# Sums of values through DRAM by blocks, and a new order of the pieces around the attention steps

## The chip, the cores and the metric

One core of a Trainium2 chip. The metric is device time in microseconds (us) of one execution. A median is over the executions of one kernel, and ratios compare fast executions of two kernels that ran in the same rounds on the same chip.

## The reference, cut to what matters

Two layers on x of 16 batches, 1024 rows and 256 columns, all in fp32. The first layer is a graph convolution with two matrix products and batch norms, a residual and a layer norm. The second one, which the change concerns, is attention whose queries come from a gated graph product:

```python
c_adj = mean(x, axis=channel)
Wg    = adj * (gate of c_adj[m] - c_adj[n])       # 1024 x 1024 per batch: the "gate rows"
g     = relu(einsum('bcn,bnm->bcm', fea, Wg) * para)   # "graph"; gives the queries
k, v  = split(x @ kv_w)                           # "keys", "values"
attn  = softmax(q @ k.T * scale)                  # 4 heads of 64
out   = attn @ v                                  # "sums of values", o
x     = layernorm(x + out)
```

## The kernel before: the parts that matter

The kernel holds scores and sums of values with the head's channels on the partitions. Each batch is 16 steps: scores of step g+1, exponentials (ScalarE), acc sums of the exponentials (VectorE), and sums of values of step g. Four steps make a turn; at the head of a turn stand "pieces", given to slots by `put(batch, slot, piece, ...)`. A turn has two slots, a batch eight. I call a batch's turns the first to the fourth. The same engine queues run scores, pieces and the preparation of the next two batches, each strictly in the order in which the program records it.

```python
def attend(g):
    ...
    if cp == NT // 2 - 1:                      # a pair of heads is complete: after 4 steps
        t = otp.tile([P, FB], F32, tag=f"ot{pair}", bufs=2 - pair, name=f"ot{g}")
        nc.scalar.copy(t, o[0]); nc.vector.tensor_add(t, o[1], t)
        OT[b, hf, pair] = t

def finish_a(b, j):                            # 64 of these: 2 x 128 rows each
    p = ps_t.tile([P, 2, C], F32, tag="t", name="pf")
    for a in range(2):
        for pair in range(NP):
            nc.tensor.transpose(p[:, a, ts(pair, P)], OT[b, hf, pair][:, ts(k + a, P)], ident)
    nc.vector.tensor_mul(r, p, rd)             # divide by the softmax sum (views cut here)
    (nc.gpsimd if b < B - 1 else nc.vector).tensor_add(r, r, x1s.pop((b, j)))
...
WG = (2, 3, 2, 1)        # gate rows per slot
QG = (6, 6, 6, 7, 7)     # graph pieces per slot, the last five slots
order = (dens, recips, finish_a, finish_b, x1_v, rows, ln1_a, ln1_b, put_x1, get_x1, finish_s, means, load, crow)
```

`dens` (tile pd) needs all acc sums of a half batch. `finish_s` takes the layer norm statistics of r, `finish_b` scales and stores the result, `means` and `crow` (tile pc) prepare the next batch's gate, `load` and `bn2_q` fetch and scale the rows of the batch after it.

## Time and profile before

| quantity | before |
|---|---|
| time, median | 2536.4 us (4 runs, 2535.86 to 2539.2) |
| span of the profiled run | 2538.7 us |
| TensorE, VectorE, ScalarE, GpSimd busy | 97%, 70%, 41%, 35% |
| a batch in the steady part | 104.10 us |
| first to fourth turn | 25.24, 24.93, 27.33, 26.61 us |

A turn is measured between the starts of its first TensorE group and the next turn's first group, averaged over twelve batches. That distance is cost on TensorE; the durations in its rows overlap and are not. The lines themselves are in the prediction.

### The profile page before, as it was taken

What the parts mean: (1) busy time and instruction counts of PE and PEld (TensorE: products, weight loads), DVE (VectorE), ACT (ScalarE), POOL (GpSimd) and SP (SyncE); (2) the same over time, 40 slices, a digit from 0 to 9 for tenths busy, and PEclk for the clock granted to TensorE, in tenths of its full rate; (3) what the DMA queues carried; (4) which work ended last, traced back from release to release, by engine and by line L of the source; (5) the groups of instructions that cost most, each with busy time, mean ns of one, the idle gap of its engine ahead of it and who ended that gap; (6) DMA issues with size and microseconds to landing.
All of it is one profiled execution on the core that took longest, in us unless ns stands there. A gap on an engine that the chain in (4) does not pass through costs nothing. (4 is left out here: it accounts for less than half of the span.)

```text
span 2538.7 us, 33394 instructions
## 1 busy us (share of the span) xinstructions
PE 2471.2 (97%) x12573; PEld 1048.0 (41%) x12573; DVE 1765.1 (70%) x2654; ACT 1042.9 (41%) x1325; POOL 876.9 (35%) x766
## 2 busy tenths in 40 slices
PE   8999999998998799999999999999999999999997
PEld 4444444443444333443434434444444344443432
DVE  5545554556767676877778778788687786877656
ACT  2000000004452355463554645646455465554644
POOL 2222223222565222433334324344243342432132
PEclk9999999999999899999999999999999999999998
DMA  3122212230785322223222221232222312222000
GB/s 133 66 83 100 100 66 83 100 115 38 273 326 183 60 57 59 51 59 67 47 55 59 58 64 43 55 69 53 63 46 54 76 38 63 47 59 63 9 14 23
DMA packets 392711, 195.27 MB, mean 77 GB/s; under 512 B 265320, under 2 KB 380640, under 8 KB 385376
## 3 DMA queue, kind: packets, MB, share of 16 engines
q1 hardware_dynamic: 392544, 193.08, 27.0%
q8 instruction: 101, 1.65, 0.3%
q14 instruction: 66, 0.54, 0.1%
HBM read 114.31 MB, written 78.71 MB: 76 GB/s over the span
## 5 line engine op out<-in xcount | busy, mean ns | idle before, releaser
L775 ACT ACTIVATE e<-s 128x1024 f32<-128x1024 f32 x512 | 496.3, 1020 | 537.1 <-PE s L763 488.5
L784 DVE TENSOR_TENSOR acc<-acc,e 128x1024 f32<-128x1024 f32 x384 | 522.2, 1360 | 73.1 <-ACT e L775 41.7
L763 PE MATMUL s<-qT,kT 64*64 64x512 f32 x4096 | 495.6, 599 | 14.8 <-ACT e L775 13.3
L794 PE MATMUL o<-e,v 64*64 64x512 f32 x4096 | 486.8, 590 | 0.0
L737 PE MATMUL pg<-wg,x 128*128 128x512 f32 x960 | 429.0, 595 | 0.0
L846 POOL TENSOR_TENSOR r<-r,x 128x512 f32<-128x512 f32 x60 | 115.7, 1928 | 555.5 <-DVE r L841 352.2
L763 PEld LDWEIGHTS s<-qT,kT 64*64 64x64 f32 x4096 | 147.7, 133 | 312.1 <-issue 251.3
L794 PEld LDWEIGHTS o<-e,v 64*64 64x64 f32 x4096 | 157.1, 133 | 285.1 <-issue 276.5
L602 POOL TENSOR_TENSOR yt<-yt,stq 128x512 f32<-128x512 f32 x120 | 188.6, 1572 | 248.5 <-DMA yt<-yT 243.8
L737 PEld LDWEIGHTS pg<-wg,x 128*128 128x128 f32 x960 | 175.5, 190 | 207.8 <-issue 198.2
L101 ACT COPY u<-pa 128x512 f32<-128x512 f32 x15 | 8.8, 586 | 475.3 <-PE pa L306 475.3
L704 DVE SCALAR_TENSOR_TENSOR wg<-wg,adj_sb 128x1024 f32<-128x1024 f32 x128 | 156.6, 1241 | 57.3 <-ACT wg L700 55.0
L306 PE MATMUL pa<-AhT,x 128*128 128x512 f32 x360 | 161.8, 592 | 0.0
L712 PE MATMUL pk<-x1T,kvw 128*128 128x512 f32 x256 | 118.4, 606 | 1.3 <-DVE x1T L663 1.3
L862 ACT ACTIVATE r<-r,nm,rs_z 128x256 f32<-128x256 f32 x128 | 69.8, 594 | 121.2 <-POOL nm L854 121.2
L723 PE MATMUL pv<-kvw,x1T 128*128 128x256 f32 x512 | 115.8, 380 | 0.8 <-ACT kT L715 0.8
L337 PE MATMUL ph<-agg,SW 128*128 128x512 f32 x240 | 112.8, 592 | 0.0
L306 PE MATMUL pa<-T,sx 128*128 128x512 f32 x240 | 107.9, 592 | 0.0
L745 DVE TENSOR_TENSOR qT<-pg,para_sb 128x512 f32<-128x512 f32 x64 | 44.2, 690 | 86.9 <-PE pg L737 86.9
L306 PEld LDWEIGHTS pa<-AhT,x 128*128 128x128 f32 x360 | 68.4, 190 | 86.1 <-issue 86.1
L723 PEld LDWEIGHTS pv<-kvw,x1T 128*128 128x128 f32 x512 | 94.9, 190 | 14.6 <-ACT kT L715 1.6
L482 PE MATMUL po<-hL,SV 128*128 128x512 f32 x224 | 98.4, 592 | 0.0
(193 smaller groups left out, 3113.6 us busy)
## 6 DMA issues: line engine op xcount, KB each, us to landing
h<-hT SPq DMA_DIRECT2D x28, 1024.0 KB, 4.4
hL<-h SPq DMA_DIRECT2D x28, 1024.0 KB, 9.4
x<-in_x_dram SPq DMA_DIRECT2D x16, 1024.0 KB, 7.2
yT<-y SPq DMA_DIRECT2D x64, 256.0 KB, 2.6
out_dram<-r SPq DMA_DIRECT2D x64, 256.0 KB, 2.2
xr<-in_x_dram SPq DMA_DIRECT2D x62, 256.0 KB, 2.9
yt<-yT SPq DMA_DIRECT2D x240, 64.0 KB, 2.2
x<-x SPq DMA_DIRECT2D x120, 128.0 KB, 2.0
```

The source lines that it names most:

```text
L306: nc.tensor.matmul(p, xs[n][:, k, :], bs[n][:, k, :], start=(k == 0), stop=(k == KN - 1))
L337: nc.tensor.matmul(p, ws[n][:, ts(f, P)], bs[n], start=True, stop=True)
L602: nc.gpsimd.tensor_tensor(y, y, sc, op)
L704: nc.vector.scalar_tensor_tensor(t, t, 1.0, adj_sb[:, i, :], op0=OP.add, op1=OP.mult)
L712: nc.tensor.matmul(p, kvw[:, k, ts(c, P)], x1Ts[b][:, k, ts(h, FB)], start=(k == 0), stop=(k == CT - 1))
L723: nc.tensor.matmul(p[:, ts(a, C)], x1Ts[b][:, k, ts(j + a, P)], kvw[:, k, C:], start=(k == 0), stop=(k == CT - 1),)
L737: nc.tensor.matmul(pg[b], x1s[b, k // 2][:, k % 2, ts(c, P)], wgs[b, k][:, ts(h, FB)], start=(k == 0), stop=(k == NT - 1))
L763: nc.tensor.matmul(t[r * HD : (r + 1) * HD, h, :], kTs[b, pair][h * HD : (h + 1) * HD, ts(2 * cb + r, HD)], qTs[b, pair, hf][h * HD : (h + ...
L775: nc.scalar.activation(E[g, a], S.pop((g, a)), AF.Exp)
L784: nc.vector.tensor_add(ACC[b, hf, pair], ACC[b, hf, pair], E[g, a])
L794: nc.tensor.matmul(O[b, hf, pair][r][h * HD : (h + 1) * HD, :], vs[b][r * HD : (r + 1) * HD, cb, pair * P + h * HD : pair * P + (h + 1) * HD],
L846: (nc.gpsimd if b < B - 1 else nc.vector).tensor_add(r, r, x1s.pop((b, j)))
```

## The change

Its intent: take the transposes of the sums of values off TensorE, by writing the sums to DRAM and fetching them back in 32x32 blocks, which VectorE can turn; and place pieces so that an engine does not stand behind another's result. The core of the diff (DRAM declarations, comments and helper lines cut):

```diff
-                t = otp.tile([P, FB], F32, tag=f"ot{pair}", bufs=2 - pair, name=f"ot{g}")
+                t = otp.tile([P, FB], F32, tag=f"ot{pair}", bufs=1, name=f"ot{g}")
...
-                OT[b, hf, pair] = t
+                if by_pe(b, hf):                 # b == B - 1 and hf == NH - 1
+                    OT[b, hf, pair] = t
+                else:
+                    nc.sync.dma_start(o_dram[b, hf][:, ts(pair, P), :]..., t...)
+        def fetch_o(b, j):
+            t = OB[b, j] = otp.tile([P, 2, C], F32, tag="ob", bufs=1, name=f"ob{b}_{j}")
+            for q in range(NQ):                  # four fetches of 32x32 blocks
+                nc.sync.dma_start(t[q * Q : (q + 1) * Q]..., blk[q][:, ts(k // 2, 2 * C // Q), :])
         def finish_a(b, j):
...
+                p = r
+                nc.vector.transpose(r, OB.pop((b, j)))
...
-        WG = (2, 3, 2, 1)
+        WG = (3, 3, 2)
-        QG = (6, 6, 6, 7, 7)
+        QG = (4, 6, 5, 5, 6, 6)
+                    put(b, t + k, fetch_o, b, hf * (KB // 2) + k)
-                    late = NC - t - 2 - k if b == B - 1 and hf == 0 else 0
+                    late = 0 if b == B - 1 else 1     # finish_b one slot later
+                    if b == B - 1 and hf == 0:
+                        late = NC - t - 2 - k
+                if b == 1:
+                    put(b - 2, j + 4, x1_t, b, j)     # batch 1: by TensorE, not DRAM
+                    continue
-                put(b - 2, j + 4, get_x1, b, j)
-                put(b - 2, j + 5, x1_v, b, j)
+                put(b - 2, 5 + j // 2 * 2, get_x1, b, j)
+                put(b - 2, min(6 + j, NC), x1_v, b, j)
-                    put(b - 1, t, wg_a, b, i)
-                    put(b - 1, t, wg_b, b, i)
+                    put(b - 1, t, gate, b, i)         # wg_b stands two rows behind wg_a
```

In slots with graph pieces the gate rows now stand in front.

More of the change, by code (lines that the diff above doesn't have):

```diff
@@ L83, in gnn_norm_attention_kernel @@
     y_blk = [yT_all[b].rearrange("i (d e) (q n) -> q e (i d) n", e=Q, q=NQ) for b in range(B)]
+    o_dram = {(b, h): dram.tile([NT // NH, C, P], F32, name=f"o{b}_{h}") for b in range(B) for h in range(NH)}
     x1_dram = {
-        (b, j): dram.tile([CT, 2 * P, P], F32, name=f"x1_{b}_{j}") for b in range(1, B) for j in range(NT // 2)
+        (b, j): dram.tile([CT, 2 * P, P], F32, name=f"x1_{b}_{j}") for b in range(2, B) for j in range(NT // 2)
     }
@@ L704, in wg_b, with gate @@
             nc.vector.scalar_tensor_tensor(t, t, 1.0, adj_sb[:, i, :], op0=OP.add, op1=OP.mult)
+        def gate(b, i):
+            wg_a(b, i)
+            for k in range(i - 2, i + 1) if i == NT - 1 else (i - 2,):
+                if k >= 0:
+                    wg_b(b, k)
         def keys(b, c, h):
@@ L784, in sums, with by_pe @@
                     nc.vector.tensor_add(ACC[b, hf, pair], ACC[b, hf, pair], E[g, a])
+        def by_pe(b, hf):
+            return b == B - 1 and hf == NH - 1
         def attend(g):
@@ L806, in attend @@
                 nc.vector.tensor_add(t, o[1], t)
-                OT[b, hf, pair] = t
+                if by_pe(b, hf):
+                    OT[b, hf, pair] = t
+                else:
+                    nc.sync.dma_start(
+                        o_dram[b, hf][:, ts(pair, P), :].rearrange("i p n -> p i n"),
+                        t.rearrange("p (i n) -> p i n", n=P),
+                    )
         def dens(b, hf):
@@ L830, in recips @@
             )
+        OB = {}
+        def fetch_o(b, j):
+            hf, k = divmod(2 * j, KB)
+            if by_pe(b, hf):
+                return
+            t = OB[b, j] = otp.tile([P, 2, C], F32, tag="ob", bufs=1, name=f"ob{b}_{j}")
+            blk = o_dram[b, hf].rearrange("i (d e) (q n) -> q e (i d) n", e=Q, q=NQ)
+            for q in range(NQ):
+                nc.sync.dma_start(
+                    t[q * Q : (q + 1) * Q].rearrange("p a (d n) -> p (a d) n", n=Q),
+                    blk[q][:, ts(k // 2, 2 * C // Q), :],
+                )
         def finish_a(b, j):
             hf, k = divmod(2 * j, KB)
-            p = ps_t.tile([P, 2, C], F32, tag="t", name="pf")
-            for a in range(2):
-                for pair in range(NP):
-                    nc.tensor.transpose(p[:, a, ts(pair, P)], OT[b, hf, pair][:, ts(k + a, P)], ident)
             pool_r = (rp, "r") if b < B - 1 else (x1p, "x1")
             r = pool_r[0].tile([P, 2, C], F32, tag=pool_r[1], name=f"r_{b}_{j}")
+            if by_pe(b, hf):
+                p = ps_t.tile([P, 2, C], F32, tag="t", name="pf")
+                for a in range(2):
+                    for pair in range(NP):
+                        nc.tensor.transpose(p[:, a, ts(pair, P)], OT[b, hf, pair][:, ts(k + a, P)], ident)
+            else:
+                p = r
+                nc.vector.transpose(
+                    r.rearrange("p a c -> p (a c)"), OB.pop((b, j)).rearrange("p a c -> p (a c)")
+                )
             rd = RD[:, b * NT + 2 * j : b * NT + 2 * j + 2, :].rearrange("p a h -> p (a h)")
@@ L953, in fast, with is_short @@
         nsteps = B * NS
-        order = (dens, recips, finish_a, finish_b, x1_v, rows, ln1_a, ln1_b, put_x1, get_x1, finish_s, means, load, crow)
+        order = (dens, recips, x1_t, finish_a, fetch_o, finish_b, x1_v, rows, ln1_a, ln1_b, put_x1, get_x1, finish_s, means, load, crow)
         rank = {f: k for k, f in enumerate(order)}
-        short = (dens, recips, finish_a, crow)
+        short = (dens, recips, x1_t, crow)
+        def is_short(fa):
+            f, a = fa
+            return f in short or f is finish_a and by_pe(a[0], 2 * a[1] // KB)
         long = (keys, values, graph)
@@ L971, in arrange @@
             first = [fa for fa in pieces if fa[0] is dens]
-            gate = [fa for fa in pieces if fa[0] in (wg_a, wg_b)]
+            gates = [fa for fa in pieces if fa[0] is gate]
             many = [fa for fa in pieces if fa[0] in long]
             first += [fa for fa in pieces if fa[0] is bn2_q]
-            few = [fa for fa in pieces if fa not in first + gate + many]
+            few = [fa for fa in pieces if fa not in first + gates + many]
             few.sort(key=lambda fa: rank.get(fa[0], len(rank)))
-            few_pe = [fa for fa in few if fa[0] in short]
+            few_pe = [fa for fa in few if is_short(fa)]
             order = spread(many, few_pe) if len(many) < len(few_pe) else spread(few_pe, many)
@@ L983, in arrange @@
             for fa in few:
-                if fa[0] not in short:
+                if not is_short(fa):
                     at_ = 0
@@ L989, in arrange @@
                     order.insert(at_, fa)
-            pairs = [gate[k : k + 2] for k in range(0, len(gate), 2)]
-            res = spread(order, pairs) if order else pairs
-            flat = []
-            for o in res:
-                flat += o if isinstance(o, list) else [o]
-            return first + flat
+            if any(fa[0] is graph for fa in many):
+                return first + gates + order
+            return first + spread(order, gates)
         nm0 = {}
@@ L1083, in fast @@
             now = [p for s in (2 * t, 2 * t + 1) for p in [(opening, (s,))] + arrange(at.get(s, []))]
-            behind = max((k + 1 for k, fa in enumerate(now) if fa[0] in short), default=0)
+            behind = max((k + 1 for k, fa in enumerate(now) if is_short(fa)), default=0)
             for k in range(len(now) + 1):
```

## The prediction

> **What bounds the kernel now.** I read the page first (engine shares, then the 40 slices), then TensorE's timeline inside one batch of the attention stage, then the list of waits, and last ScalarE's timeline at the one place where TensorE waits every batch. The shares and slices:
>
> ```profile
> PE 2471.2 (97%) x12573; PEld 1048.0 (41%) x12573; DVE 1765.1 (70%) x2654; ACT 1042.9 (41%) x1325; POOL 876.9 (35%) x766
> ...
> PE   8999999998998799999999999999999999999997
> ```
>
> TensorE is full in nearly every slice. The change touches the attention stage, from about 860 us on. There a batch takes 104 us, in four turns of four steps. A step is 16 matmuls of scores (s) and 16 of sums of values (o); other pieces stand at the head of each turn. Columns: start, duration, engine, line, operation, tiles, count:
>
> ```profile
> 1518.26 1.07 PE L815 MATMUL pd<-acc,ones 128*32 128x512 f32 x8
> 1519.25 3.70 PE L712 MATMUL pk<-x1T,kvw 128*128 128x512 f32 x8
> 1522.79 0.60 PE L826 MATMUL pr<-ident,dt 128*128 128x128 f32 x4
> 1523.23 3.60 PE L712 MATMUL pk<-x1T,kvw 128*128 128x512 f32 x8
> 1526.66 0.60 PE L837 MATMUL pf<-ident,ot 128*128 128x128 f32 x4
> 1527.10 1.89 PE L723 MATMUL pv<-kvw,x1T 128*128 128x256 f32 x8
> 1528.92 1.95 PE L763 MATMUL s<-qT,kT 64*64 64x512 f32 x16
> 1530.69 1.90 PE L794 MATMUL o<-e,v 64*64 64x512 f32 x16
> 1532.97 2.01 PE L763 MATMUL s<-qT,kT 64*64 64x512 f32 x16 [0.39 <-ACT e L775]
> ...
> 1568.42 2.12 PE L815 MATMUL pd<-acc,ones 128*32 128x512 f32 x8
> ```
>
> Durations overlap, so cost is the distance between starts. Four pf transposes cost 0.44 us (1526.66 to 1527.10), not 0.60. The usual step is 1.72 + 1.72 us. Two flaws recur: s at 1532.97 starts 2.28 us after o, 0.56 more than usual, and pd at 1568.42 takes 2.05 us to the next group, against 0.99. The waits that repeat or are large:
>
> ```profile
> PE s L763 <- ACT e L775: 13.3, 16, 4.8
> ...
> PEld pd L815 <- DVE acc L784: 12.9, 14, 1.0
> ...
> PE pc L683 <- DVE cs L666: 9.8, 1, 9.8
> ```
>
> (total us, times, longest). Comparing every start distance from 900 us on with the median of its kind leaves only 44 us of lost time: 8 us in 14 of the 0.56 us flaws, 14 us in pd, 8.3 us in two single waits (3.3 before the scores at 908, 5.0 at 2475), the rest crumbs. All else is work. ScalarE's side of the first flaw:
>
> ```profile
> 1519.39 0.59 ACT L817 COPY dt<-pd 128x512 f32<-128x512 f32 x1 [0.44 <-PE pd L815]
> 1519.87 1.15 ACT L699 ACTIVATE wg<-crow,cs 128x1024 f32<-128x1024 f32 x1
> 1521.05 1.06 ACT L700 ACTIVATE wg<-wg 128x1024 f32<-128x1024 f32 x1
> 1522.02 0.57 ACT L715 COPY kT<-pk 128x512 f32<-128x512 f32 x1
> 1522.99 0.59 ACT L715 COPY kT<-pk 128x512 f32<-128x512 f32 x1 [0.41 <-PE pk L712]
> ...
> 1531.91 1.93 ACT L775 ACTIVATE e<-s 128x1024 f32<-128x1024 f32 x2
> ```
>
> In the first turn of a batch ScalarE is solid with gate rows and copies, so the exponentials of a score finished near 1529.8 begin only at 1531.91, and the next scores find no free buffer.
>
> **What the Trainium skill says.** "TensorE: Matmul & The Clock Gate", Part 4, gives about 275 ns for a transpose in a kernel. This trace's median is 273 ns, but consecutive starts are 109 ns apart, and that spacing is the cost. The same page, in the paragraph on engine queue depths, calls ScalarE and VectorE strict FIFO; the trace agrees, the exponentials above run only behind the gate rows. "VectorE: DVE Perf Modes", The three transpose paths, says VectorE transposes 32x32 blocks only, which is why the blocks must be moved by DMA. The stream transposes here take 705 ns for 128x512. "DMA: Bandwidth & Descriptors", Anatomy of one DMA, gives about 2 us fixed for a transfer on the GpSimd path. Here 64 KB block fetches, issued by SyncE, land in 2.2 us.
>
> **The change, part by part.**
>
> *Transposes leave TensorE.* Of 64 pieces with four pf transposes, 62 now go by DRAM and VectorE (the last half of the last batch stays). 62 x 0.44 = 27 us off TensorE's path. VectorE gains 62 x 0.705 = 44 us on 1765; it is off the path where it has room. Batch 1's x1 goes back to TensorE (16 transposes, 1.7 us), in the opening where TensorE waits anyway.
>
> *The opening.* Before, VectorE waits 5.75 us at 874.6 and 5.15 us at 883.8 for batch 1's xb fetches, ahead of the last layer-norm rows, so crow's transpose is 9.8 us late (885.6). Without those fetches I place it near 881: GpSimd's last scaling ends at 872.8, rows and statistics take 2.6, scaling and means 3, and x1's transposes sit between the last matmuls of the opening. The row's DMA is issued only at 890.60 behind twelve xb issues, and its gate starts at 896.50. With a free queue the same 5.9 us from issue to gate give about 887.6. ScalarE then has 10.9 us of work before the next exponentials, plus 1.05 for one more gate row: 899.5 against 907.4. About 8 us gained.
>
> *Gate rows in front.* The second half of a gate row now stands two rows behind its ScalarE half, ending VectorE's 55.0 us of waits on wg; that is not on TensorE's path. But the first turn now holds six gate rows, not five, and the output scaling of the previous batch's second quarter (two activations, 1.0 us) slips into it. By start distances, an even row is 2.14 us (1.18 + 0.96), an odd one 1.05, a copy 0.47. ScalarE from pd's start: 1.12 until dt, 0.49 dt, 1.0 output, 3 x 2.14 + 3 x 1.05 = 9.57 gates, 5 x 0.47 = 2.35 copies: exponentials at 14.5 us. Before: 1531.91 - 1518.26 = 13.65, including 0.93 us of waits for pk that disappear when more gate work is in front. So scores resume about 0.87 us later than before, although TensorE's own pieces became 0.44 us shorter. The pf saving of this turn is lost and 0.87 added: 14 x 1.31 = +18 us.
>
> *The late dens (pd).* Per batch VectorE's second turn lasts as long as TensorE's (1545.2 to 1569.4, against 25.0), so the last acc is 1.05 us late. In the new order TensorE's second turn has ten graph pieces in place of six (+3.4 us, less the removed 0.5), VectorE's about +2 (one more gate row, one transpose). The lateness should vanish mostly: -11 of 14 us.
>
> *The tail.* The 5 us wait at 2475 comes from output scaling that holds ScalarE until GpSimd and VectorE have finished the rows; one slot later it no longer does: -5. But in the last four turns almost no long pieces remain, and VectorE now stands for the round trip: sums written (about 2.5), fetched (four issues of 0.5 and 2.2), so data about 8 us after the turn's start, where the first acc sum is done at 5.8. Then the acc of the turn pair ends late, I estimate 4 us, once before each of the two last dens: +8. Net +3.
>
> Sum: -27 - 8 + 18 - 11 + 3 = -25 us; 2536.6 - 25 = 2512. I round to 2511.
>
> **Rivals.** First, everything wins: the ScalarE load of the first turn does not grow, the 0.56 us flaw goes, pd's waits and the tail vanish. Then -27 - 8 - 14 - 8 - 5 = -62, 2475 us. For it speaks that VectorE's waits fall everywhere; against it, ScalarE's list above, which is already solid and gets longer. Second, VectorE becomes the bound: at 78% of the span between 1100 and 1500 it gains 2.8 us a batch, and in the third turn TensorE's work shrinks by over 3 us to about 23.7, where VectorE needs about 23.3. If its waits for the fetched sums stack up there, TensorE's waits for acc move rather than vanish: +1 us a batch, 2525 or more. For it: GpSimd contention already stretches acc sums from 1.23 to 1.88 us. Against it: six exponential buffers, and the fourth turn has 5 us of slack. Third, DMA: some 20 more issues a batch at 0.5 us add 10 us to a queue that I estimate at 25 us busy of 104 (some 50 issues), and DMA's busy share is 24%, so bandwidth binds nowhere; only latency in the tail counts.
>
> **Range and chances.** The transposes are nearly certain. The ScalarE term is the largest doubt, from 0 to +30; opening and tail are each good for 5 us either way. That gives 2488 to 2527. To be faster by over 2% it must fall under 2486, nearly the whole first rival: 0.11. Slower by over 2% would need a new wait of over 5 us a batch: 0.02.
>
> **What would show it.** pf falls to 8 transposes; PE busy drops by about 25 us; s's waits on e number about 14 of 1 to 2 us each, 15 to 25 us in total, right after the first scores of each batch; pd's wait on acc falls below 5 us in the steady part; pc's 9.8 us wait shrinks to a few; VectorE's busy time rises by about 45 us. If s's waits do not grow, I misjudged ScalarE's order and the time is nearer 2490. If s or pd wait longer on acc or on fetched sums inside the steady part, the second rival holds.

## The result, and the profile after

| quantity | before | after |
|---|---|---|
| time, median | 2536.4 us | 2534.6 us (4 runs, 2533.6 to 2536.27) |
| ratio after to before | | 0.9991 (0.9974 to 1.0009) |
| a batch in the steady part | 104.10 us | 105.08 us |
| turns one to four | 25.24, 24.93, 27.33, 26.61 | 26.12, 27.86, 25.72, 25.39 |
| opening: first graph matmul to the second turn of the first batch | 72.3 us | 62.1 us |
| last dens but two to the end | 84.8 us | 80.5 us |

The result is the same within 2%, at 2534.6 us, outside the predicted range of 2488 to 2527.

The spans differ by 6.9 us (2538.7 and 2531.8), of which 4.8 arise before the first changed instruction: the opening's first graph matmul starts at 848.19 before and 843.39 after, in a stage that the change does not touch. From there to the end the difference is 2.1 us, close to the 1.8 of the medians. Its parts: the opening -10.1, fourteen batches +13.5, the last long turns -1.2, the tail -4.3.

So the transposes were removed, and each batch became longer. The shares of the engines after, from the page:

```profile
PE 2445.6 (97%) x12341; PEld 1025.0 (40%) x12341; DVE 1791.6 (71%) x2716; ACT 1037.6 (41%) x1325; POOL 786.3 (31%) x766
```

TensorE lost exactly 232 instructions (248 transposes out, 16 in) and 25.6 us of busy time, as foretold. The time did not follow: TensorE's idle time took it (67.5 us of the span before, 86.2 after). TensorE's timeline of one batch after, at the three places where it waits:

```profile
1507.76 1.06 PE L834 MATMUL pd<-acc,ones 128*32 128x512 f32 x8
...
1519.75 2.60 PE L807 MATMUL o<-e,v 64*64 64x512 f32 x16
1523.36 2.00 PE L771 MATMUL s<-qT,kT 64*64 64x512 f32 x16 [1.00 <-ACT e L783]
...
1561.73 1.05 PE L834 MATMUL pd<-acc,ones 128*32 128x512 f32 x4
1563.36 1.05 PE L834 MATMUL pd<-acc,ones 128*32 128x512 f32 x4 [0.58 <-DVE acc L792]
1564.35 4.56 PE L745 MATMUL pg<-wg,x 128*128 128x512 f32 x10
...
1587.46 5.42 PE L745 MATMUL pg<-wg,x 128*128 128x512 f32 x12
1593.61 0.27 PE L684 MATMUL pc<-ident,cs 128*8 128x128 f32 x1 [0.73 <-DVE cs L667]
```

The scores resume 15.60 us after pd's start (1523.36 - 1507.76), against 14.71 before. pd takes 2.62 us to the next group, against 2.05. And pc, which did not wait at all in the steady part before, now comes 1 us late: twelve graph matmuls at 0.43 would end at 1592.6. The same in the list of waits (total us, times, longest; PEld is TensorE's loading of weights):

```profile
DVE st_z L551 <- POOL r L885: 45.8, 18, 3.6
...
PEld pd L834 <- DVE acc L792: 34.1, 27, 2.7
...
PE s L771 <- ACT e L783: 17.9, 15, 3.1
...
PE pc L684 <- DVE cs L667: 10.2, 14, 0.7
```

Before, the first of these was 21.1 us in 18 waits of at most 1.2 us; the weight load of pd waited 12.9 us. A batch's account: TensorE's work fell by 1.88 us (0.44 or 0.50 per transpose piece, four a batch). The first turn's score wait cost 1.32 more than the transposes' absence allowed (25.24 - 0.44 to 26.12), pd 0.55 more (27.33 - 0.44 - 1.72 of moved graph work to 25.72), pc 1.00 (26.61 - 0.50 - 1.72 to 25.39). That is -1.88 + 2.87 = +0.99, the measured +0.98.

**Where pd's lateness comes from.** I follow it back through four queues in the first turn of that batch. SyncE's queue after, then GpSimd's, then VectorE's (an idle time in brackets stands for the wait before the row):

```profile
1509.20 0.38 SPq L823 DMA_DIRECT2D o<-ot  x1
1511.50 1.91 SPq L860 DMA_DIRECT2D ob<-o  x4
1513.51 0.44 SPq L904 DMA_DIRECT2D out_dram<-r  x1
1513.99 2.13 SPq L436 DMA_DIRECT2D yt<-yT  x4
```

```profile
1518.89 2.96 POOL L603 TENSOR_TENSOR yt<-yt,stq 128x512 f32<-128x512 f32 x2 [28.63 <-DVE r L880]
1521.81 1.27 POOL L885 TENSOR_TENSOR r<-r,x 128x512 f32<-128x512 f32 x1
```

```profile
1518.60 1.22 DVE L705 SCALAR_TENSOR_TENSOR wg<-wg,adj_sb 128x1024 f32<-128x1024 f32 x1
1523.11 0.43 DVE L551 BATCH_NORM_STATS2 st_z<-r 128x6 f32<-128x256 f32 x1 [3.29 <-POOL r L885]
...
1554.12 9.19 DVE L792 TENSOR_TENSOR acc<-acc,e 128x1024 f32<-128x1024 f32 x6
```

The loads of the batch after next (yt) stand behind the write and the fetches of the sums, so they are issued 6.2 us after pd. Before, they ran ahead of the turn:

```profile
1504.42 1.98 SPq L435 DMA_DIRECT2D yt<-yT  x4
```

That is 13.8 us before that batch's pd at 1518.26. GpSimd scales these rows first and adds the residual after it, and the releaser named in its first row (the product r, at 1517.39) is only the last event by the profile; the semaphores it waits for include the loads, the last of which lands at 1518.51. VectorE then stands 3.29 us at the statistics of r. From 1523.11 on it has no idle time until the last acc sum before pd ends (1554.12 + 9.19 = 1563.31, and pd's second half starts at 1563.36), so the stand arrives at pd undiminished. A queue that stands shows as nothing: SyncE has no row between 1509.58 and 1511.50. The Trainium skill says this of the profile ("Perfetto Trace Analysis", DMA Instruction — HWDGE): the semaphore wait comes before the window that the profiler reports. The gap in SyncE's rows here agrees.

**The opening and the tail.** In the opening, pc stood at 885.63 after a 9.82 us wait; after:

```profile
874.20 0.60 PE L663 MATMUL px<-ident,x 128*128 128x128 f32 x4
874.63 0.27 PE L684 MATMUL pc<-ident,cs 128*8 128x128 f32 x1
874.84 1.09 PE L771 MATMUL s<-qT,kT 64*64 64x512 f32 x8
```

In the tail the 5 us wait before the scores is gone, but pd waits for acc before each of the last two dens:

```profile
2481.30 1.05 PE L834 MATMUL pd<-acc,ones 128*32 128x512 f32 x4
2484.17 1.05 PE L834 MATMUL pd<-acc,ones 128*32 128x512 f32 x4 [1.82 <-DVE acc L792]
```

### The profile page after: what moved, and what is told of

Read it like the earlier page. It is cut to its first block, busy times and chain, and to the rows that moved or that the text cites. A ratio compares the mean times of both kernels' runs of the same rounds, so it can differ in the third digit from the quotient of the medians.

```text
span 2531.8 us, 33526 instructions
## 1 busy us (share of the span) xinstructions
PE 2445.6 (97%) x12341; PEld 1025.0 (40%) x12341; DVE 1791.6 (71%) x2716; ACT 1037.6 (41%) x1325; POOL 786.3 (31%) x766
## 4 chain that ended last, share of the span: by engine, by line
PE 41%; DVE 19%; issue 5%; ACT 5%; DMA 3%; POOL 2%; SPq 1%; DVEq 0%; POOLq 0%; ACTq 0%
PE s L771 11%; PE o L807 10%; PE pg L745 10%; DVE acc L792 8%; PE po L483 7%; DVE wg L705 2%; DVE x L628 2%; DMA yt<-yT 1%; PE pv L731 1%; PE pd L834 1%; ACT wg L700 1%; ACT wg L696 1%; POOL yt L603 1%; ACT wg L701 1%; DVE st_z L551 1%
## 5 line engine op out<-in xcount | busy, mean ns | idle before, releaser
L792 DVE TENSOR_TENSOR acc<-acc,e 128x1024 f32<-128x1024 f32 x384 | 508.5, 1324 | 79.9 <-ACT e L783 50.4
L771 PE MATMUL s<-qT,kT 64*64 64x512 f32 x4096 | 492.1, 595 | 18.6 <-ACT e L783 17.9
L807 PE MATMUL o<-e,v 64*64 64x512 f32 x4096 | 494.7, 589 | 0.0
L603 POOL TENSOR_TENSOR yt<-yt,stq 128x512 f32<-128x512 f32 x120 | 169.4, 1412 | 459.2 <-DMA yt<-yT 304.9
L885 POOL TENSOR_TENSOR r<-r,x 128x512 f32<-128x512 f32 x60 | 76.4, 1274 | 451.5 <-issue 380.3
L819 DVE TENSOR_TENSOR ot<-o,ot 128x512 f32<-128x512 f32 x64 | 44.0, 687 | 74.7 <-ACT ot L818 74.7
L467 ACT ACTIVATE hL<-hL,t,s 128x512 f32<-128x512 f32 x112 | 79.7, 802 | 25.0 <-DMA hL<-h 25.0
```

The costliest lines, as they stand in the source:

```text
L603: nc.gpsimd.tensor_tensor(y, y, sc, op)
L771: nc.tensor.matmul(t[r * HD : (r + 1) * HD, h, :], kTs[b, pair][h * HD : (h + 1) * HD, ts(2 * cb + r, HD)], qTs[b, pair, hf][h * HD : (h + ...
L792: nc.vector.tensor_add(ACC[b, hf, pair], ACC[b, hf, pair], E[g, a])
L807: nc.tensor.matmul(O[b, hf, pair][r][h * HD : (h + 1) * HD, :], vs[b][r * HD : (r + 1) * HD, cb, pair * P + h * HD : pair * P + (h + 1) * HD],
```

## The experiments

My theory: three separate waits, each at the head of one in-order queue, ate the 27 us. One is on ScalarE in the first turn, one runs SyncE, GpSimd, VectorE to pd, one is on VectorE ahead of pc. The rival: VectorE's or ScalarE's amount of work now paces the batch, so any order only moves the wait. Twelve kernels ran, all correct. Each ratio is against the kernel before. To compare two variants I take the difference of their ratios or medians; the kernel before was between 2536.4 and 2538.1.

**Means ahead of statistics (pc).**

```diff
-order = (..., put_x1, get_x1, finish_s, means, load, crow)
+order = (..., put_x1, get_x1, means, finish_s, load, crow)
```

> The changed kernel with one order changed: the means of the next batch stand ahead of the output statistics instead of behind them. Theory (three queues, each in order, hold TensorE once a batch): the transpose pc waits 0.9 to 1.0 us in each of 15 batches because the two pairs of statistics (1.2 us on VectorE) stand ahead of the means; this wait goes, pc's wait on cs falls to under 2 us in total, and the time falls by 12 to 14 us, to about 2521. Rival (VectorE's amount of work paces the batch, an order only moves the wait): pc's wait goes but pd's wait on acc or s's wait on e grows by as much, and the time stays within 4 us of 2534.6.

Measured 2522.1 us, ratio 0.9942. pc directly follows its graph matmuls:

```profile
1582.96 5.42 PE L745 MATMUL pg<-wg,x 128*128 128x512 f32 x12
1588.22 0.27 PE L684 MATMUL pc<-ident,cs 128*8 128x128 f32 x1
```

The fourth turn fell from 25.39 to 24.50 us, the other turns stayed (26.11, 27.86, 25.54). So a change of VectorE's order alone removed this wait.

**Output scaling out of the first turn (ScalarE).**

```diff
-                    late = 0 if b == B - 1 else 1
+                    late = 0 if b == B - 1 or (hf == 0 and k == 1) else 1
```

> The changed kernel with the output scaling of a batch's second block back in the fourth turn, out of the next batch's first turn. Theory: ScalarE's queue in the first turn gets 1.0 us shorter, so the exponentials start 1.0 us earlier and the 1.18 us loss before the third scores falls to about 0.2 us; 14 times 1.0 = 14 us, to about 2521. Rival (ScalarE is kept by something else in that turn, the copies that wait for TensorE): the loss stays above 0.8 us and the time within 4 us of 2534.6.

Measured 2522.8 us, ratio 0.9945; the first turn fell from 26.12 to 25.14, by 0.98. The third scores start 14.63 us after pd (1503.32) in place of 15.60:

```profile
1517.95 2.00 PE L771 MATMUL s<-qT,kT 64*64 64x512 f32 x16 [0.74 <-ACT e L783]
```

**Loads ahead of the fetches (pd).**

```diff
-                put(b - 2, j, load, b, j)
+                put(b - 2, j, load_now if j < 2 else load, b, j)     # load_now calls load
-order = (dens, recips, x1_t, finish_a, fetch_o, finish_b, x1_v, rows, ...)
+order = (dens, recips, x1_t, finish_a, x1_v, load_now, fetch_o, finish_b, rows, ...)
```

> The changed kernel with the next batch's first two row loads ahead of the fetches of the sums in SyncE's queue. Theory (chain of queues): the loads wait behind the fetch of the sums, so GpSimd's scaling and then its addition come late, and VectorE stands 3.3 us in the first turn before the output statistics; with the loads in front that idle falls under 1 us, acc is done at least 1 us earlier at the second turn's end, pd's loss falls from about 1.6 to about 0.5 us or less, and the time falls by 12 to 20 us, to 2515 to 2523. Rival (VectorE simply has 27 us of work in the second turn): pd's loss stays at 1.3 us or more and the time falls by less than 5 us.

Measured 2520.3 us, ratio 0.9931. Its waits:

```profile
PEld pd L834 <- DVE acc L792: 10.3, 12, 2.7
...
DVE st_z L551 <- POOL r L885: 7.2, 5, 1.4
```

VectorE's stand at the statistics is gone (45.8 to 7.2 us in total) and with it most of pd's (34.1 to 10.3). The third turn fell from 25.72 to 24.61.

**The residual addition on VectorE (pd again, by another link of the chain).**

```diff
-            (nc.gpsimd if b < B - 1 else nc.vector).tensor_add(r, r, x1s.pop((b, j)))
+            (nc.gpsimd if b < B - 1 and j != 2 else nc.vector).tensor_add(r, r, x1s.pop((b, j)))
```

> The changed kernel with the residual addition of the first turn's block (one of four per batch) on VectorE instead of GpSimd; loads stay where they are. Theory (VectorE stands behind GpSimd's late addition in the first turn): that stand of about 3.3 us per batch goes for 0.7 us of work, acc is ready earlier, pd's loss falls from 1.6 to under 0.8 us a batch and the time falls by 9 to 18 us, to 2517 to 2526. Rival (the stand is harmless, the loads' place helped for another reason): pd's loss stays and the time stays within 4 us of 2534.6.

Measured 2519.5 us, ratio 0.9930, third turn 24.47 us. VectorE got more work and the kernel became faster, with loads as late as before. So the amount of VectorE's work alone does not make pd late; the stand ahead of it does, and the loads acted through GpSimd's addition. The amount is a condition, though: VectorE works without a gap from the stand to pd, so it cannot make the lost time good.

**All three orders.** The edits of the means, the scaling and the loads together.

> All three orders of the runs before it at once. Theory: the three losses are separate waits of TensorE and add up, about 14 + 14 + 12 to 20 us, so 2488 to 2498. Rival (VectorE's or ScalarE's amount of work paces the batch): the sum of the three single gains is not reached, less than 20 us in all, over 2514.

Measured 2502.0 us, ratio 0.9858. In ratios the three single gains are 0.0049, 0.0046 and 0.0060, in sum 0.0155; together they gave 0.0133, 86% of it. pd still waits (third turn 25.17, against 24.61 with the loads alone), because VectorE has less time when the first turn is shorter: it enters the second turn 1.92 us after TensorE, with the loads alone 1.40 (means of twelve batches). The next run tests this. So neither extreme holds: most of each gain stays, and a little comes back.

**One graph piece from the third turn to the second.** On top of the three orders:

```diff
-        QG = (4, 6, 5, 5, 6, 6)
+        QG = (5, 6, 5, 4, 6, 6)
```

> The three orders at once, and one graph piece of 0.86 us moved from the third turn to the second, so that VectorE has more time before the sums of the first half. Theory: the 0.5 us that pd still loses in the third turn of each batch (second turn's acc late) goes, 6 to 8 us in 14 batches, to about 2495; the third turn has room, its lateness is absorbed by the fourth. Rival (VectorE then falls behind in the third turn and TensorE waits there or at pc): within 3 us of the run with the three orders, 2502.

Measured 2491.5 us, ratio 0.9819. It was 10 us faster than the three orders, a little more than expected: pd had lost 0.8 us a batch, not 0.5, since the second and third turn together fell from 53.02 to 52.23.

**The sums by TensorE again, in the new order.** The removed part put back, the rest of the change kept:

```diff
-            return b == B - 1 and hf == NH - 1      # by_pe
+            return True
-                t = otp.tile([P, FB], F32, tag=f"ot{pair}", bufs=1, ...)
+                t = otp.tile([P, FB], F32, tag=f"ot{pair}", bufs=2 - pair, ...)
```

> The changed kernel, in its new order, with the sums of values turned by TensorE again (the removed part put back, 248 transposes). Theory (the trip through DRAM is what fills the queues): TensorE gets 27 us more work, but the loads no longer wait behind the fetches and VectorE loses 62 transposes, so pd's and pc's losses shrink by 14 to 24 us; the time is 2537 to 2549, so the trip is worth only 3 to 14 us as it stands. Rival (the trip costs nothing beside TensorE's path and the other moves are to blame): 27 us more, about 2562.

Measured 2515.9 us, ratio 0.9916. Both expectations missed: with its 248 transposes back on TensorE the kernel is 19 us faster than the change. The trip through DRAM had not merely failed to pay; as placed, it cost more than the transposes. Its turns are 26.11, 28.25, 24.57, 24.90. The first turn is as long as with the trip, 26.12, although it has a transpose piece more: the scores start 15.59 us after pd at 1502.68 in either case, set by ScalarE.

```profile
1518.27 2.00 PE L771 MATMUL s<-qT,kT 64*64 64x512 f32 x16 [1.26 <-ACT e L783]
```

In the other three turns the transposes add 0.39 to 0.50 each, while pd's and pc's waits vanish. I had put these waits at 14 to 24 us and the transposes at 27. But a quarter of the transposes was hidden behind ScalarE, and near the end the trip costs 3 us more (80.5 against 77.5).

**The same with the three orders, and with the moved graph piece.** The previous edit on top of those two kernels.

> The three orders at once with the sums of values turned by TensorE again. Theory: with the queues in order the removed transposes are on TensorE's path nearly whole, so this is 15 to 27 us slower than the three orders with the trip through DRAM, 2517 to 2529. Rival (VectorE's work paces the batch, and the removed TensorE time only turns into waits): under 8 us slower.

Measured 2503.8 us, ratio 0.9864, only 2 us slower than the three orders with the trip: the expectation missed and the rival's number held. In the steady part the trip saves only 0.14 us a batch there (102.68 against 102.82). The first turn, set by ScalarE, is as long either way (25.13 and 25.12), and in the third pd's wait for VectorE's sums costs more than the transposes (25.17 against 24.56). So with the queues in order the rival is right in part: TensorE still waits for VectorE's work. The tail takes back 3.9 us (81.5 against 77.6), and 2.7 us of gain stand in the opening (62.0 against 64.7), which no run explains.

> The orders of the best version with all sums of values turned by TensorE: what is the trip through DRAM worth once no queue holds it up? Theory: with TensorE's transposes no wait of TensorE on acc is left that the moved graph piece could mend, so this stays at the 2503.8 of the three orders with TensorE's transposes, within 3 us, and the trip (kept out of the tail) is worth 14 to 20 us of its 27. Rival (the gain of the last two steps was the moved graph piece alone): 2490 or less.

Measured 2502.9 us, ratio 0.9862, as expected: without the trip nothing of TensorE's waits on acc is left for the moved piece to mend.

**The second batch's x1 by TensorE, alone, on the kernel before.**

```diff
+                if b == 1:
+                    put(b - 2, j + 4, x1_t, b, j)
+                    continue
                 put(b - 2, j + 3, put_x1, b, j)
-order = (dens, recips, finish_a, ...
+order = (dens, recips, x1_t, finish_a, ...
-short = (dens, recips, finish_a, crow)
+short = (dens, recips, x1_t, finish_a, crow)
```

> The kernel before with one part of the change alone: the second batch's x1 is turned by TensorE, not sent through DRAM. Theory: from the first graph matmul to the first pv of the second batch's steady turns the changed kernel was 10 us shorter than the kernel before, and this part is its whole cause, so 8 to 11 us less than the kernel before, 2526 to 2529. Rival (the gain there comes from the new places of the other pieces): under 4 us.

Measured 2527.8 us, ratio 0.9960. The opening takes 62.2 us (845.25 to 907.41), just as in the changed kernel. This part is the whole gain of the opening, 10 us.

**The output scaling later, alone, on the kernel before.** The edit of `late` from the change.

> The kernel before with one part of the change alone: the output scaling one slot later. Theory: the 5 us wait near the end goes, but the first turn's ScalarE queue gets 1.0 us longer and TensorE's pieces there are as before, so the loss before the third scores grows from 0.56 to about 1.5 us in 14 batches: 14 times 0.95 minus 5 is 8 us slower, about 2545. Rival (ScalarE absorbs it in its idle time for pk): no more than 0.2 us a batch, about 2533.

Measured 2536.1 us, ratio 0.9993: the rival was right on the first turn, which stayed at 25.23, but a batch grew by 0.43 us, more than its 0.2. ScalarE's row for the first two copies shows how, with no wait for pk in front of the second, where the kernel before had waited 0.41:

```profile
1522.60 1.05 ACT L715 COPY kT<-pk 128x512 f32<-128x512 f32 x2
```

Two activations more are free in the old order, which had 0.93 us of idle ScalarE time there, and cost 0.98 a batch in the new one, whose sixth gate row fills that time first. The tail fell from 84.8 to 77.4 us, so this part is the cause of the tail's gain. The second turn rose from 24.93 to 25.37, in a wait of its last two graph matmuls for VectorE's half of a gate row:

```profile
1553.81 1.13 PE L737 MATMUL pg<-wg,x 128*128 128x512 f32 x2 [0.60 <-DVE wg L704]
```

By the traces, ScalarE's first gate row starts 2.61 us after pd (1.61 before), and VectorE is still 0.74 us later when it comes to that row in the second turn. No run tests this link.

**The best version.** The moved graph piece and the three orders, and TensorE's transposes for the last three half batches, where nothing covers the trip:

```diff
-            return b == B - 1 and hf == NH - 1
+            return b == B - 1 or b == B - 2 and hf == NH - 1
+                if b == B - 1 and hf == 0 and pair == 0:
+                    t = otp.tile([P, 2, C], F32, tag="ob", bufs=1, ...)   # in the block buffer's place
```

> The best version so far (three orders, one graph piece moved) with the sums of the last three half-batches turned by TensorE, where no long pieces cover the trip through DRAM. Theory: from the fourth-last dens to the end the versions with the trip take 80.5 to 81.5 us and those with TensorE's transposes 77.5, so 4 us less than that version, about 2487.5; the two waits of pd on acc near the end (1.8 and 1.6 us) go. Rival (the end is paced by something else): within 1.5 us of 2491.5.

Measured 2486.4 us (2485.23 to 2487.65), ratio 0.9798, interval 0.9782 to 0.9814, so it is faster, but whether by 2% is unclear. The tail takes 77.3 us in place of 81.5, and dens stands undivided where the changed kernel had waited:

```profile
2439.23 1.07 PE L837 MATMUL pd<-acc,ones 128*32 128x512 f32 x8
2441.01 0.66 PE L848 MATMUL pr<-ident,dt 128*128 128x128 f32 x4 [0.71 <-ACT dt L839]
```

Against the same orders with all transposes on TensorE (2502.9) the trip is here worth 16.5 us. Its 58 pieces (64 less the six of the last three half batches) take about 26 us off TensorE, at 0.44 each.

| kernel | median us | ratio | turns one to four | batch |
|---|---|---|---|---|
| before | 2536.4 | 1 | 25.24, 24.93, 27.33, 26.61 | 104.10 |
| the change | 2534.6 | 0.9991 | 26.12, 27.86, 25.72, 25.39 | 105.08 |
| change, sums by TensorE | 2515.9 | 0.9916 | 26.11, 28.25, 24.57, 24.90 | 103.82 |
| change, three orders | 2502.0 | 0.9858 | 25.13, 27.85, 25.17, 24.52 | 102.68 |
| and the moved graph piece | 2491.5 | 0.9819 | 25.13, 28.71, 23.52, 24.59 | 101.95 |
| and the tail by TensorE | 2486.4 | 0.9798 | 25.14, 28.71, 23.47, 24.57 | 101.89 |

## Why the prediction was wrong

The prediction was 2511 (2488 to 2527); measured were 2534.6. "Same within 2%" was its likeliest class, but the size and the reason failed.

- **Transposes, -27:** right on TensorE's work. Its busy time fell by 25.6 us, and the steady turns show 0.44 to 0.50 us for each piece.
- **ScalarE in the first turn, +18:** right in size. The turn rose by 0.88 us where 0.87 was foretold, the exponentials began 14.52 us after pd (1522.28) where 14.5 was foretold, and the scaling run took 0.98 of it back. One thing in the working was too coarse: the run on the kernel before shows that the scaling alone would have been free in this turn. With the sixth gate row alone (the scaling run) the scores start 14.63 us after pd, as early as before (14.71); only the row and the scaling together move them.
- **The late dens, -11:** this is the step that failed. It said "The lateness should vanish mostly". It grew by 0.55 us a batch, about +8 in fourteen batches, 19 us off. I compared only the amounts of VectorE's and TensorE's work in the second turn. I had not asked when VectorE enters that turn. The fetches put the loads 6.2 us behind pd, GpSimd's addition comes late, and VectorE, which has no idle time from there to pd, stands 3.3 us. Moving the loads (third turn -1.1 us) and moving the addition (-1.25) each showed it, so some 15 of the 19 us lie there. The rest is a size: by the traces VectorE works 27.0 us from its entry into the second turn to pd's last sum, before 24.2, so 2.8 more and not 2 (TensorE's turn grew by 2.9, as foretold). The third rival in the prediction held that the new DMAs' latency counts "only" in the tail; that was the same mistake, since it weighed the queue's total time and not its order. By the prediction's own last test the second rival (VectorE becomes the bound) holds: pd's wait on acc did not fall but rose (12.9 to 34.1 us over the whole run), and a batch grew by 0.98 where that rival said 1. The number is partly luck: it is the sum of four terms, and pd's share is 0.55. VectorE does lack slack before pd, but the stand for GpSimd's addition in the first turn, which the rival does not name, makes it late.
- **A missing step:** the wait of pc. VectorE began the means 5.86 us after the turn's start in place of 5.07, because the block transpose (0.7 us) now stands ahead of them, and TensorE's part of the turn before pc became 1.36 us shorter (one graph piece and one transpose piece fewer). Before, there were 1.3 us between the means and pc; after, pc came 1 us late, +14 us in fourteen batches. The means run took 0.89 of it away per batch. My sum had no such term.
- **The opening, -8:** right in mechanism, measured -10.1, and the run with that part alone gives all of it.
- **The tail, +3:** measured -4.3. The scaling gained 7.4, not 5, and the two late dens cost less than my 8: about 3, by the 80.5 us against 77.5 with TensorE's transposes.

In sum, dens and pc put 33 us on the prediction, and opening and tail took 9 off: 2512 + 33 - 9 = 2536, against 2534.6. Of the test lines that I had set, "s's waits on e number about 14, 15 to 25 us in total" held (15 waits, 17.9 us), and VectorE's busy time rose by 26 us, not 45. Of the missing 19, 15 are acc sums: 53 of them, in place of 80, took more than 1.5 us, and in both traces each of these overlaps GpSimd's scaling of rows (1324 ns on average after, 1360 before).

What stays open: how the later scaling delays VectorE's gate row in the old order, which only the traces show, and why the opening is 2 to 3 us longer in the two kernels that have the three orders and TensorE's transposes.

## What to carry to other kernels

When work is moved off the bounding engine, follow each new instruction into the queue where it will stand, and ask what stood behind it there: here the cost that I missed was not the time of the new DMAs, but loads, an addition and a row of means that had to queue behind them, on a VectorE that had no slack to make it good. A queue that used to run ahead, such as the loads here, has slack that no busy share shows, and a dependent transfer placed in front of it spends that slack. Put the removed part back inside the new schedule as an experiment: it separates the value of the idea (16.5 us) from the price of its placement (19 us the other way).

## What the Trainium skill lacked or had wrong

- "TensorE: Matmul & The Clock Gate", Part 4: its figure of about 275 ns for a transpose in a kernel (beside one for bf16 in isolation) is the duration of one; it gives no spacing. Transposes in a row cost 109 ns each from start to start here (fp32, 128x128, four in 0.44 us, with a duration of 273), and that is what removing one saves.
- "DMA: Bandwidth & Descriptors", Issuing engines are not separate DMA queues, calls the time on the sequencer to start a DMA usually small beside the DMA. A fetch of a 64 KB block here held SyncE for 0.48 us (four in 1.91) and landed in 2.2. That the issuing sequencer itself waits is stated (the HWDGE section above); no page that I read draws from it that a fetch waiting for an earlier write stops unrelated loads behind it. Here they went from 13.8 us ahead of pd to 6.2 us behind it.
